# Four fused convolution layers on one core: the half products are issued in pairs, and one without a partner waits for the next quarter

## The chip, the cores and the metric

The kernel runs on one core of one Trainium2 chip. The metric is device microseconds of one execution, lower is better. Three runs of the kernel before gave 2782.89, 2783.59 and 2784.94 us, a median of 2783.59 us.

## The reference

The input is x of 16 images, 64 channels, 128 by 128 pixels, all float32. Four layers follow each other, each of them x = x + f(groupnorm(x)) with 32 groups of two channels:

```
x = x + conv_w @ (gram(xn) @ xn)           # gram = xn xn^T / 16384, 64x64 per image
x = x + |scharr_x(xn)| + |scharr_y(xn)|    # per channel, 3x3
x = x + conv3x3(shifted(xn), W) + b        # a quarter of the channels one pixel left, one right
x = x + clip(leaky(batchnorm(conv1x1(conv3x3(xn, w_bin), w1x1))), 0, 255)
```

The batch norm takes its mean and variance over all 16 images, so the last step of layer 3 can only start when every image has passed the third convolution.

## The kernel before

**Tiles.** A tile holds 128 partitions. In the front (layers 0 and 1) these are 64 channels times the two halves of the image's rows; in the convolutions they are 64 channels times even and odd rows. A tile covers 16 rows, so an image takes NS = 8 steps. The three stages `Front`, `Layer2` and `Layer3` run at the same time on different images, one tile each in a step; `Layer2` is 10 steps and `Layer3` 20 steps behind `Front` (`starts`, line 922). A fourth piece, `Gram`, turns a later image's rows into columns (`rows_to_columns`, ScalarE) and forms the 64x64 Gram matrix with 128 small products of 65 columns (`gram_product`, line 406). From it `gram_chain` computes the coefficients of layer 0 in some nine links, each with small products (`small_product`, line 171) that go into the PSUM tile `bank`; `coefficients` does the same for the group norms of layers 2 and 3 with one small product each. A link of a chain is run by `tick()` at the end of a quarter.

**Order.** A step has four quarters q = 0 to 3. In the loop of line 972 each quarter runs, in this order: the "first of" pieces, `Layer3`, `Layer2` and `Front` for the images that are in them, the "last of 3" piece in quarter 3, `Gram`, and `tick()`. All engines except the queues' own work keep the program's order (`InOrder`, line 63): an instruction never passes another one of its engine in the instruction stream.

**Halves on TensorE.** Almost every product has 128 rows of weights and 64 columns; it writes PSUM partitions 0 to 63 (half 0) or 64 to 127 (half 1). The variable `last[0]` is the half of the last product issued. `small_product` issues one product for each half, beginning with the other half than the last. `issue` (line 652) takes two lists, one for each half, and alternates; when one list is used up it issues the rest of the other.

**A convolution tile.** `shared` issues three products for each half into `one`. `own` (line 672) issues for one of the two output row sets five products into `two`: three taps for one half, and two products for the other, because one of its two is packed with the twin tile `qd` (`pk`). So one half has one product more. For `Layer2`, `own(…, 1, …)` in quarter 2 has the extra product in half 0 and `own(…, 0, …)` in quarter 3 has it in half 1. For `Layer3` the two calls are in quarters 0 (extra in half 0) and 1 (extra in half 1). Line 803 to 825 and 880 to 886 hold these calls.

**The inputs of `own`.** `difference(name, n, t)` (line 634, VectorE) writes `d2[:, n]` or `d3[:, n]`; there is one buffer for each n. The difference of `Layer2` for n = 1 is written in "last of 3" (line 830), at the end of quarter 3, for the next tile; it overwrites what the three taps of quarter 2's `own` read. The twin `qd` is a shifted copy of `d`, made by two transfers from the GpSimd queue for layer 2 and by ScalarE for layer 3.

**Other names of the profile.** `po` is the product of layer 0 for half a tile (quarters 1 and 3), from which ScalarE makes the normalized `xh`. VectorE writes `y` (layer 3's output, quarter 2) from `two` and the bias tile `c`, and `x` written from `two,c` is layer 2's output (quarter 0); `two<-two,edges` are the two border corrections ahead of the latter. The Gram products of an image stand in three parts of 44, 42 and 42 (line 477 and, for images 1 to 6, line 499). For images 7 to 15 the parts are in quarter 0 and 2 of one step and quarter 0 of the next.

**After the convolutions.** When the last tile of layer 3 is done, the batch norm's coefficients are formed, and the loop of line 1056 reads `y_d` and `x3_d` back, applies the last step and writes the output.

All instructions issued through `InOrder` carry line 73 in the profile, so groups are told apart by the tiles that they write and read.

Of the kernel before, what the change touches and what calls it, by code (L numbers as in the profile page):

```python
# [108 lines left out]
def tile_kernel(ctx: ExitStack, tc: tile.TileContext, x, cw_h, w2_t, b2, wbin_t, w1_t, b1, gamma, beta, consts, out):  # L109
    nc = tc.nc  # L110
    pe, dve, act, sp, pool = (InOrder(tc, e) for e in (nc.tensor, nc.vector, nc.scalar, nc.sync, nc.gpsimd))
# [57 lines left out]
    last = [1]  # L169
# [55 lines left out]
    def weights_of_layer_3(ky):  # L225

        pw = bank[C:P, 512 - 3 * C:512].rearrange("p (k c) -> p k c", k=3)
        for kx in range(3):
            pe.matmul(pw[:, kx, :], wb[:, ky, kx, :], w1, start=True, stop=True)
        for slot, i, o, kk in TO_PAIRS:  # L230
            if kk == ky:
                act.copy(w3[i * C:(i + 1) * C, slot, :, o * C:(o + 1) * C], pw)
# [5 lines left out]
    def other_weights():  # L238
        for n in range(2):
            o = 1 - single(TO_SLOTS, n)[0]  # L240
            pool.tensor_copy(wm[:, :, cols(o)], w2[:, n, :, cols(o)])

        for name, w, table in (("pk2", w2, TO_SLOTS), ("pk3", w3, TO_PAIRS)):
            dve.tensor_add(w[:, 2], w[:, 0], w[:, 1])
            packed[name] = wpool.tile([P, 2, C], F32, name=name)
            for n in range(2):
                o, i = single(table, n)
                for kx, half in ((1, i), (0, 1 - i)):
                    pool.tensor_copy(
                        packed[name][half * C:(half + 1) * C, n], w[i * C:(i + 1) * C, n, kx, o * C:(o + 1) * C]  # L250
                    )
# [4 lines left out]
    def tick():  # L256
        for c in list(chains):
            if next(c, chains) is chains:
                chains.remove(c)
# [146 lines left out]
    def gram_product(pg, w):  # L406

        s = w % 2
        pe.matmul(
            pg[s * C:(s + 1) * C, :], xw[:, w // 2, 0:C, s], xw[:, w // 2, :, s],  # L410
            start=(w < 2), stop=(w >= W - 2),
        )
        last[0] = s

    def rows_to_columns(b, m, t):
        act.copy(
            xw[:, :, m * C // 8:(m + 1) * C // 8, :].rearrange("p w c t -> p c w t"),
            t.rearrange("p c (w t) -> p c w t", t=2),
        )
# [38 lines left out]
    class Gram:  # L458
        first, last = 0, NS + 1
# [21 lines left out]
        def part(self, n):  # L481
            if self.w == 0 and n:
                self.pg = ps_g.tile([P, CP, W], F32, tag="g", name=f"pg_{self.b}")[:, 0, 0:C + 1]
            for _ in range(n):
                gram_product(self.pg, self.w)
                self.w += 1

        def load(self, m):
            t = xin.tile([P, C // 8, W], F32, tag="xr", name=f"xr_{self.b}_{m}", bufs=3)
# [17 lines left out]
    class Front:  # L507
        first, last = -3, NS
# [132 lines left out]
    def taps(o, p, wts, srcs, pad=0):  # L641
# [7 lines left out]
                ))  # L649
        return made  # L650

    def issue(halves):

        n = [0, 0]
        while n[0] < len(halves[0]) or n[1] < len(halves[1]):
            o = 1 - last[0]
            if n[o] == len(halves[o]):
                o = last[0]
            dst, wt, src = halves[o][n[o]]
            n[o] += 1  # L660
            pe.matmul(dst, wt, src, start=(n[o] == 1), stop=(n[o] == len(halves[o])))
            last[0] = o

    def products(p, wts, srcs):
        issue([taps(o, p, wts, srcs) for o in range(2)])
# [6 lines left out]
    def own(p, n, table, wt, name, m=CP, both=None):  # L672
        d, q, pk = diffs[name][:, n, 0:m], twins[name][:, n, 0:m], packed[f"pk{name[1]}"][:, n]
        o, _ = single(table, n)
        some = [None, None]
        some[1 - o] = taps(1 - o, p[:, 0:m], [wt[:, n] if both is None else both], [d], 1)
        some[o] = [
            (p[cols(o), 0:m], pk, q[:, :, 1:1 + W]),
            (p[cols(o), 0:m, 0:W - 1], wt[:, n, 2, cols(o)], d[:, :, 2:1 + W]),
        ]  # L680
        issue(some)
# [4 lines left out]
    class Layer2:  # L686
        first, last = -2, NS
# [146 lines left out]
    class Layer3:  # L834
        first, last = -1, NS
# [89 lines left out]
    def run(stage, b, i, q):  # L925
        if 0 <= b < B and stage.first <= i <= stage.last:
            if (stage, b) not in live:
                live[stage, b] = stage(b)
            live[stage, b].at(i, q)
# [20 lines left out]
    def rest(pool, tag, shape, bufs, n=None):  # L950
        for m in range(bufs if n is None else n):
            t = pool.tile([P] + shape, F32, tag=tag, name=f"end_{tag}_{len(room)}", bufs=bufs)
            while len(t.shape) > 2:
                t = t.rearrange("p a b c -> p (a b) c" if len(t.shape) == 4 else "p a b -> p (a b)")
            room.append(t[:, 0:N])

    def slices(t, n):
        room.extend(t[:, j * N:(j + 1) * N] for j in range(n))
# [3 lines left out]
    def fetch():  # L962
        n = fetched[0]
        if n < len(parts):
            b, q = parts[n]
            yt, rt = room.popleft(), room.popleft()
            sp.dma_start(yt, whole(y_d[b], q))
            sp.dma_start(rt, whole(x3_d[b], q))
            loaded.append((yt, rt))
            fetched[0] += 1  # L970

    for step in range(starts[2][1] - 2, steps):
        for q in range(4):
            for b in range(B):

                i = step - starts[2][1] - NS * b
                if 0 <= i < NS and q in (0, 2):
                    live[Front, b].sobel(i, f"first of {q}")
                if q == 3:
                    run(Layer2, b, step - starts[1][1] - NS * b, "first of 3")  # L980
            for stage, at in starts:
                for b in range(B):
                    run(stage, b, step - at - NS * b, q)
            if q == 3:
                for b in range(B):
                    run(Layer2, b, step - starts[1][1] - NS * b, "last of 3")
            for b in range(1, B):
                at, n = pace[b]
                if n == 1:
                    run(Gram, b, step - at, q)  # L990
                elif 0 <= step - at <= 5:
                    live.setdefault((Gram, b), Gram(b)).half(4 * (step - at) + q)

            first = starts[2][1]
            if step == first and q < 3:
                rows_to_columns(1, NS - 3 + q, rows[NS - 3 + q])
            if q == 1 and first + 2 <= step < first + 5:
                weights_of_layer_3(step - first - 2)
            if q == 1 and step == first + 5:
                other_weights()  # L1000
            tick()

            if step == last_one - NS and q == 0:
                slices(xw.rearrange("p w c t -> p (w c t)"), 8)
                slices(xh.rearrange("p a j w -> p (a j w)"), 3)
                rest(xin, "x", [R, W], 2)
                rest(xin, "xr", [C // 8, W], 3)
                rest(work, "u", [R + 1, W + 2], 2)
                rest(work, "e", [R, W + 2], 1)
            if step == last_one and q == 0:  # L1010
                rest(ring, "v2", [(R + 1) * W + 2], 3)
                for t in (diffs["d2"], twins["d2"]):
                    slices(t.rearrange("p n j w -> p (n j w)"), 1)
            if step >= last_one and q == 2:

                n = 3 if step == last_one else 1 if step < last_one + NS - 2 else 0
                rest(ring, "x3", [2, CP, W], NS + 2, n)

            if step >= last_one - NS and q == 3 and len(room) > 1:
                fetch()  # L1020
# [82 lines left out]
```

## Time and profile before

| | |
|---|---|
| median of three runs | 2783.59 us |
| the profiled execution's own time | 2780.96 us |
| its span, first to last instruction | 2779.2 us |
| TensorE matmul busy | 2220.0 us (80%) |
| VectorE busy | 2193.7 us (79%) |
| ScalarE busy | 2113.9 us (76%) |
| GpSimd busy | 837.1 us (30%) |
| products of 64 columns, rows of the profile | 14804, two for each product |
| last product of the convolutions | near 2326 us of the span |
| from there to the end | reading back, last step, writing out |

The busy shares are those of the whole span. From about 316 us (first tile of layer 3) to about 2053 us all three stages run; the profile before that is the filling of the pipeline, after it the emptying. From 2340 us on TensorE is idle and the 16 transfer engines are fully busy (414 GB/s). A timeline row gives the start, the length, the engine, the operation, the tiles, the shape, the number of merged instructions and, in brackets, the engine's idle time before it and what ended it. A product leaves two rows, one for each of two passes; the length of a row includes about 0.16 us in which the next product already runs, so the start of the next row tells more than the length.

### The profile page before, as it was taken

The numbers are of one execution on the slowest core, as the hardware profiler recorded it, in microseconds if no ns is written. First come the engines' busy times: TensorE is split into PE (matmuls) and PEld (weight loads), VectorE is DVE, ScalarE is ACT, GpSimd is POOL, SyncE is SP. The second block draws the span as 40 slices with busy tenths as digits, with TensorE's granted clock in tenths as the row PEclk, the third lists the DMA queues.
The fourth block names the chain that finished last, engine by engine and source line by source line (L and its number), as shares of the span: only waits on it lengthen the run. The fifth ranks groups of instructions, "written<-read, shape, count | busy, mean of one in ns | idle before, by whom it ended". The sixth has DMA issues, their size and how long they took to land. (4 is left out here: it accounts for less than half of the span.)

```text
span 2779.2 us, 46241 instructions
## 1 busy us (share of the span) xinstructions
PE 2220.0 (80%) x14804; PEld 1125.6 (41%) x14804; DVE 2193.7 (79%) x3623; ACT 2113.9 (76%) x3177; POOL 837.1 (30%) x1350
## 2 busy tenths in 40 slices
PE   6478899999999999999999999999999995000000
PEld 4234444545454535453535353566666641000000
DVE  5999999898989898989898989999996435333332
ACT  4766889898989898989898988999997667333332
POOL 2054434332333242324242424444444300000000
PEclk8689999999999999999999999999999997555555
DMA  7789888888888888888888867787877768999999
GB/s 200 201 226 233 231 208 232 227 220 221 216 227 223 221 221 222 220 227 215 226 218 223 218 181 204 205 215 208 213 201 188 216 192 285 419 420 420 420 420 390
DMA packets 680289, 685.97 MB, mean 247 GB/s; under 512 B 60096, under 2 KB 580448, under 8 KB 680048
## 3 DMA queue, kind: packets, MB, share of 16 engines
q1 hardware_dynamic: 654896, 613.83, 74.5%
q0 software_dynamic: 25152, 69.18, 10.2%
q8 instruction: 120, 1.97, 0.3%
q14 instruction: 121, 0.99, 0.1%
HBM read 346.23 MB, written 268.44 MB: 221 GB/s over the span
## 5 line engine op out<-in xcount | busy, mean ns | idle before, releaser
L73 PE MATMUL two<-d,w 128*64 128x508 f32 (+2 forms) x2560 | 884.4, 586 | 0.0
L73 PE MATMUL two<-d,wi 128*64 128x508 f32 (+3 forms) x1536 | 616.6, 577 | 0.0
L73 POOL DMA_DIRECT2D qd<-d x512 | 270.8, 531 | 900.5 <-issue 382.2
L73 PE MATMUL two<-qd,pk 128*64 128x512 f32 (+1 forms) x1024 | 518.2, 587 | 5.9 <-DMA qd<-d 5.4
L73 POOL TENSOR_SCALAR edges<-v,co 64x8 f32<-64x8 f32 x512 | 308.4, 602 | 370.4 <-ACT v L73 276.3
L73 PEld LDWEIGHTS two<-d,w 128*64 128x64 f32 x2560 | 299.3, 136 | 279.9 <-issue 202.8
L73 PE MATMUL one<-v,wi 128*64 128x508 f32 (+3 forms) x1536 | 396.6, 596 | 2.5 <-issue 2.5
L73 PE MATMUL one<-v,w 128*64 128x508 f32 (+2 forms) x1600 | 398.1, 578 | 0.5 <-ACT c L73 0.5
L73 PE MATMUL po<-x,abd 128*64 128x512 f32 x1024 | 351.9, 617 | 51.9 <-ACT xh L73 48.9
L73 DVE TENSOR_TENSOR d<-v 128x512 f32<-128x512 f32 (+1 forms) x512 | 346.0, 679 | 38.6 <-ACT qd L73 14.2
L73 ACT COPY qd<-d 64x512 f32<-64x512 f32 x512 | 315.4, 616 | 21.1 <-DVE d L73 14.6
L73 ACT ACTIVATE xh<-po,co 128x128 f32<-128x128 f32 (+1 forms) x480 | 275.1, 621 | 63.7 <-PE po L73 60.5
L73 DVE SCALAR_TENSOR_TENSOR e<-e 128x1032 f32<-128x1032 f32 (+1 forms) x256 | 313.0, 1223 | 0.0
L73 DVE SCALAR_TENSOR_TENSOR y<-two,c 128x1024 f32<-128x1024 f32 x128 | 156.0, 1219 | 133.5 <-ACT v L73 66.4
L73 PEld LDWEIGHTS two<-d,wi 128*64 128x64 f32 x1536 | 193.9, 135 | 153.0 <-issue 109.9
L73 ACT ACTIVATE v<-x,co 128x512 f32<-128x512 f32 (+2 forms) x368 | 234.9, 704 | 0.0
L73 PEld LDWEIGHTS one<-v,w 128*64 128x64 f32 x1600 | 162.3, 137 | 176.3 <-issue 119.7
L73 POOL TENSOR_SCALAR v<-v,kc 128x9 f32<-128x9 f32 x256 | 228.2, 905 | 11.9
L73 PEld LDWEIGHTS one<-v,wi 128*64 128x64 f32 x1536 | 157.2, 139 | 161.6 <-issue 120.0
L73 ACT ACTIVATE u<-u 128x1024 f32<-128x1024 f32 x128 | 135.1, 1055 | 65.3 <-DVE u L73 65.3
L73 DVE SCALAR_TENSOR_TENSOR u<-xh 128x1170 f32<-128x1170 f32 x128 | 175.6, 1372 | 4.7 <-ACT xh L73 3.8
L73 PEld LDWEIGHTS two<-qd,pk 128*64 128x64 f32 x1024 | 130.2, 136 | 111.6 <-issue 72.1
(162 smaller groups left out, 3453.8 us busy)
## 6 DMA issues: line engine op xcount, KB each, us to landing
x<-in_x SPq DMA_DIRECT2D x256, 256.0 KB, 4.0
x_d<-u SPq DMA_DIRECT2D x512, 128.0 KB, 3.7
y_d<-y SPq DMA_DIRECT2D x512, 128.0 KB, 4.1
x_d<-x SPq DMA_DIRECT2D x496, 128.0 KB, 2.5
xr<-in_x SPq DMA_DIRECT2D x120, 512.0 KB, 6.5
qd<-d POOLq DMA_DIRECT2D x256, 130.0 KB, 3.0
qd<-d POOLq DMA_DIRECT2D x256, 129.8 KB, 3.7
v<-x_d SPq DMA_DIRECT2D x448, 72.1 KB, 3.0
```

The costliest lines, as they stand in the source:

```text
L73: return self.tc.keep_in_program_order(call(*args, **kwargs))
```

## The change

`issue` no longer issues everything. Each half has a queue (`held`). `issue` puts its products at the end of the queues, with their start and stop flags, and then issues pairs, one product for each half, as long as both queues hold something. A product without a partner stays in its queue until the next `issue`. Before `Front` in quarters 1 and 3 `issue_rest` would empty the queues. The parts of the Gram are issued in pairs that begin with the other half than the last.

```diff
-            for _ in range(n):
-                gram_product(self.pg, self.w)
-                self.w += 1
+            for _ in range(n // 2):
+                for s in (1 - last[0], last[0]):
+                    gram_product(self.pg, self.w + s)
+                self.w += 2
...
+    held = [deque(), deque()]
+
+    def emit(o):
+        dst, wt, src, start, stop = held[o].popleft()
+        pe.matmul(dst, wt, src, start=start, stop=stop)
+        last[0] = o
+
     def issue(halves):
 
-        n = [0, 0]
-        while n[0] < len(halves[0]) or n[1] < len(halves[1]):
+
+        for o in range(2):
+            for n, (dst, wt, src) in enumerate(halves[o]):
+                held[o].append((dst, wt, src, n == 0, n + 1 == len(halves[o])))
+        while held[0] and held[1]:
             o = 1 - last[0]
-            if n[o] == len(halves[o]):
-                o = last[0]
-            dst, wt, src = halves[o][n[o]]
-            n[o] += 1
-            pe.matmul(dst, wt, src, start=(n[o] == 1), stop=(n[o] == len(halves[o])))
-            last[0] = o
+            emit(o)
+            emit(1 - o)
+
+    def issue_rest():
+        while held[0] or held[1]:
+            emit(1 - last[0] if held[1 - last[0]] else last[0])
...
             for stage, at in starts:
+                if stage is Front and q in (1, 3):
+                    issue_rest()
                 for b in range(B):
                     run(stage, b, step - at - NS * b, q)
```

The number of instructions on every engine stays the same, and the order on VectorE, ScalarE, GpSimd and the queues too. On TensorE the third product of `own` in quarters 0 and 2 now stands behind the Gram part and the small products of that quarter's `tick()`, as the first product of the next quarter; where nothing stands between, the order of products is the one of before.

## The prediction

> **What bounds the kernel now.** First the stretches with the busy time of each engine, to see where TensorE sets the pace.
>
> ```profile
> 400.00:600.00 200.00, 198.88 (x1268) 100.22 (x1265) 188.15 (x324) 181.56 (x284) 74.79 (x123) 1.00 0.88 231
> 1805.00:1929.00 124.00, 124.00 (x630) 79.93 (x628) 120.70 (x180) 113.95 (x181) 57.57 (x82) 1.00 0.82 210
> 2340.00:2780.00 440.00, 0.00 (x0) 0.00 (x0) 149.35 (x124) 149.50 (x122) 0.00 (x0) 0.50 1.01 414
> ```
>
> The columns are length, busy us of TensorE, weight loads, VectorE, ScalarE and GpSimd, granted clock, share of the transfer engines, GB/s. TensorE is busy all the time until the last 440 us, which transfers bound and the change doesn't touch. VectorE is busy 188 of 200 us, so a gain on TensorE may end at VectorE. So I read VectorE's waits next, around one image's Gram steps (first tile of layer 3 of that image at 860.7 us).
>
> ```profile
> 919.30 1.23 DVE L73 SCALAR_TENSOR_TENSOR y<-two,c 128x1024 f32<-128x1024 f32 x1 [1.16 <-ACT u L73]
> 924.49 0.69 DVE L73 TENSOR_TENSOR d<-v 128x512 f32<-128x512 f32 x1 [0.36 <-issue]
> 929.58 0.38 DVE L73 TENSOR_TENSOR two<-two,edges 128x8 f32<-128x8 f32 x2 [1.95 <-PE two L73]
> 939.98 1.23 DVE L73 SCALAR_TENSOR_TENSOR y<-two,c 128x1024 f32<-128x1024 f32 x1 [3.43 <-ACT junk L73]
> 945.38 0.56 DVE L73 TENSOR_TENSOR d<-v 128x384 f32<-128x384 f32 x1
> DVE d L73 <- POOL v L73: 0.4, 2, 0.2
> ```
>
> The last row is the whole list of VectorE's waits from 946 to 1055 us: 0.4 us. The image's period is 136.3 us (724.4, 860.7, 997.0 us). So it has two parts: TensorE leads up to 940 us, where VectorE waits up to 3.43 us for it; then VectorE runs without a pause for more than 100 us, and TensorE waits for it through ScalarE (`po` behind `xh`, 1.2 us at 876.7). Time is saved only if both parts hand on earlier.
>
> **Part 1: the lone product.** How TensorE treats a product without a partner:
>
> ```profile
> 1001.23 0.23 PE L73 MATMUL bank<-st,kc 128*64 128x2 f32 x2
> 1001.32 1.05 PE L73 MATMUL two<-d,w 128*64 128x512 f32 x3
> 1002.08 0.22 PE L73 MATMUL bank<-st,kc 128*64 128x2 f32 x2
> ...
> 912.93 0.34 PE L73 MATMUL pg<-xw 128*64 128x65 f32 x2
> 913.35 0.59 PE L73 MATMUL two<-d,w 128*64 128x508 f32 x1
> 913.78 2.92 PE L73 MATMUL pg<-xw 128*64 128x65 f32 x86
> 916.48 0.59 PE L73 MATMUL two<-d,w 128*64 128x512 f32 x1
> 916.53 0.59 PE L73 MATMUL two<-qd,pk 128*64 128x512 f32 x1
> ```
>
> A small product of half 1 runs at 1001.23 beside the lone product of half 0 (two passes of 0.427 us, 0.854 in all). Half 1 goes on with its next long product at 1001.32; the small one of half 0, earlier in the program, runs only at 1002.08. The halves are two streams; each loses 0.085 us at the small product and 0.033 in the long one behind it (second pass at 1001.78, 0.46 later instead of 0.427), 0.118 us.
>
> The page "TensorE: Matmul & The Clock Gate" of the Trainium skill, Part 3, says that matmuls start and end strictly in program order. By it each of the 55 small groups and 34 Gram parts that stand behind a lone product would idle a half for up to 0.854 us, and the change would gain up to 89 × 0.854 / 2 = 38 us. The rows at 1001.32 and 1002.08 contradict it, and the sum goes by them.
>
> Small products between pairs, with the halves level:
>
> ```profile
> 324.06 0.28 PE L73 MATMUL bank<-ad,cs 128*64 128x64 f32 x4
> 324.18 0.23 PE L73 MATMUL bank<-vv,abd 128*64 128x2 f32 x4
> 324.27 0.26 PE L73 MATMUL bank<-vv,wbd 128*64 128x1 f32 x4
> 324.38 1.91 PE L73 MATMUL one<-v,wi 128*64 128x512 f32 x8
> ```
>
> Three of them take 324.06 to 324.38, with the late second pass 0.356 us, against 3 × 0.118 = 0.354. So I cost moving the 55 groups at 0. Bounds: nothing, and each 0.118 dearer (the halves' small products one after the other), 55 × 0.118 = +6.5 us.
>
> **Part 2: the Gram parts.** A Gram part is not free behind a lone product: half 1 makes one Gram product at 912.93 and then waits until half 0 has finished its long one. It spends 912.93 to 916.48 = 3.55 us on 22 products; half 0 takes 913.78 to 916.53 = 2.75. So half 1 loses 0.80 us, half 0 nothing. In the changed kernel both do the part from 912.93 to 915.68, and then the pairs. Half 0 is where it was, half 1 0.80 earlier. The image's two later parts lose nothing in either half (926.82 and 926.85), as half 0 is then ahead by that much.
>
> `y` needs both halves. At 919.30 it could go 0.80 earlier (VectorE is free at 918.14), and at 939.98 0.81. This would be the gain.
>
> **Part 3: what waits for the held product.** The difference at 924.49 overwrites what the held product reads. That product runs from 923.39 (last row end 924.40, and 0.09 to the difference). Now it stands behind the Gram part of 42, 2.64 us (924.19 to 926.82): end 927.04, difference 927.13, 2.64 later. Behind it on VectorE stand `u` and `e` (3.12 us up to the end of `e`), so `two<-two,edges`, held by TensorE until 929.58, starts at 930.25: 0.67 late. The 6.98 us of work up to the next `y` then ends at 937.2, before TensorE's 939.17. The 3.43 us of wait shrink to 1.9: no cost. GpSimd's transfers behind this difference (`qd`) are 2.6 us later and are read some 15 us later: no cost.
>
> But the next difference, at 945.38, has no wait and no room. The product it overwrites is of half 0: second pass at 944.59, end 945.17, with 0.09 it is free at 945.26. Half 0 is not earlier in the changed kernel. So VectorE, 0.81 early at `y`, waits here for 0.69 and keeps 0.12. From here to 1055 us VectorE has no slack: 0.12 is what the image hands on. Nine images have this pattern (`y` with a wait near 509.6, 646.7 and so on to 1601.4): 9 × −0.12 = −1.1 us. Bounds: 0, and 9 × −0.81 = −7.3.
>
> **Part 4: the filling (166 to 370 us).** Images 4 to 6 have Gram parts in quarter 2 beside layer 2 while `y` isn't there. At 203.31 the difference waits for GpSimd; its lone product starts at 201.39. Held behind 2.75 us of Gram it ends at 205.16, the difference goes at 205.25, 1.94 late, and `two<-two,edges` goes at 208.4 instead of 207.71: +0.7. A second part of the image adds about as much, some 1.3 us an image. In the last of the three `y` waits 3.06 us for TensorE (at 345.5), which should take it back. So 2 × 1.3 = +2.6 us; bounds 0 and 3 × 1.3 = +3.9.
>
> **Part 5: elsewhere 0.** From 1680 to 2250 us no Gram is left. TensorE is the bound (124.00 of 124.00), both halves' work stays the same, and small products cost the same 0.118 in either place. In the emptying nothing stands between the quarters' products, so the order is unchanged.
>
> **Sum.** −1.1 + 2.6 = +1.5 us. The profiled execution took 2780.96 us (span 2779.2 and 1.8 around it), which makes 2782.5. The median of the runs is 2.6 above that execution: 2785.1 us.
>
> **Rivals.**
> *Faster: half 1's 0.8 us is handed on whole.* For it: `y` waits on TensorE, and half 1 is the later one in every Gram step. Against it: the end of half 0's product at 945.17, 0.2 us ahead of the difference. If the differences held nothing up and the filling cost nothing, −7.3: 2776.3 us.
> *Slower: the held product stops VectorE for good.* Place: the difference behind the Gram part in quarter 2, 2.64 us late. It decides from the point where `y` at 939.98 has no wait left, or where ScalarE, behind VectorE's `u`, is late with `xh` and so with `po`. Then the 0.67 us at 929.58 stay in all nine images, 6.0 us, with 2.6 of the filling +8.6: 2792.2 us. Against it: 1.9 us of wait remain by my walk.
> *The change does less than it says.* Where no Gram or chain link stands between two quarters the order is unchanged, and if the waits take both signs back the time is 2783.6; this lies within my forecast.
>
> **How the numbers follow.** 0.2% is 5.6 us, about what a measurement of this kernel can tell from no change. No change within it: 0.62 (2778.0 to 2789.2). Faster: 0.17. Slower: 0.21, with the dearer small products (+6.5) in it. The forecast's own range is 2782 to 2788: filling 0 to +3.9, images 0 to −1.1, and a run's spread of 1 us. The range of 8 in 10 reaches to both rivals: 2776 to 2792.
>
> **What would show it.** In the changed profile: each Gram part in one row of 84 or 88 products, with no long product inside; `y` about 0.7 us earlier in the period than now with a wait of about 2 us at the second one; a wait of about 0.7 us at the difference that follows it; a wait of some 3 us at the difference behind the Gram part in quarter 2; periods of 136.2 us. I am wrong if the period moves by more than 0.5 us, if steps without Gram take more than 15.4 us, or if three small products between pairs take more than 0.36 us.

## The result, and the profile after

| | runs | median us | lowest to highest |
|---|---|---|---|
| kernel before, beside it | 12 | 2782.92 | 2779.74 to 2784.94 |
| changed kernel | 12 | 2782.61 | 2778.85 to 2784.50 |

The ratio is 0.9999, 95% interval 0.9991 to 1.0006: no change that can be told. The profiled execution of the changed kernel took 2783.50 us, its span 2781.7 us.

First the stretches with the busy time of each engine, of the changed kernel (columns as before):

```profile
400.00:600.00 200.00, 197.14 (x1262) 93.91 (x1260) 188.41 (x323) 183.57 (x286) 76.83 (x122) 1.00 0.88 232
1805.00:1929.00 124.00, 124.00 (x630) 80.05 (x628) 120.78 (x179) 113.99 (x182) 56.78 (x83) 1.00 0.81 210
2340.00:2780.00 440.00, 0.00 (x0) 0.00 (x0) 151.77 (x126) 151.93 (x125) 0.00 (x0) 0.50 1.02 416
```

VectorE's 188 of 200 us, TensorE's 124.00 of 124.00 without Grams and the end are what they were. Over the whole span TensorE is busy 2209.7 us instead of 2220.0 with the same 14804 rows. Two halves that are level cover less time than two of which one lags, which would fit; no run shows this by itself.

TensorE's timeline of the changed kernel around an image's Gram parts (first tile of layer 3 of this image at 1000.9 us):

```profile
1052.36 1.02 PE L73 MATMUL two<-d,w 128*64 128x508 f32 x4
1053.21 2.92 PE L73 MATMUL pg<-xw 128*64 128x65 f32 x88
1055.96 1.44 PE L73 MATMUL two<-d,w 128*64 128x512 f32 x5
...
1063.66 2.80 PE L73 MATMUL pg<-xw 128*64 128x65 f32 x84
1066.30 1.02 PE L73 MATMUL two<-d,wi 128*64 128x512 f32 x4
```

Each part is one row of 88 or 84 entries (44 or 42 products) with no long product inside. From its start to the next product the larger part takes 2.75 us and the smaller one 2.64, in both halves. Half 1's 3.55 us are gone. The held product is now the first of its half behind the part, in the row at 1066.30; its second pass ends at 1067.32.

VectorE's timeline of the changed kernel through the same steps, and from its list of waits the rows for the 106 us behind them:

```profile
1058.81 1.23 DVE L73 SCALAR_TENSOR_TENSOR y<-two,c 128x1024 f32<-128x1024 f32 x1 [0.38 <-ACT v L73]
...
1067.41 0.69 DVE L73 TENSOR_TENSOR d<-v 128x512 f32<-128x512 f32 x1 [3.74 <-issue]
...
1070.46 0.38 DVE L73 TENSOR_TENSOR two<-two,edges 128x8 f32<-128x8 f32 x2
...
1079.44 1.22 DVE L73 SCALAR_TENSOR_TENSOR y<-two,c 128x1024 f32<-128x1024 f32 x1 [2.01 <-ACT e L73]
...
1085.54 0.56 DVE L73 TENSOR_TENSOR d<-v 128x384 f32<-128x384 f32 x1 [0.61 <-issue]
DVE d L73 <- POOL v L73: 0.4, 2, 0.2
```

The waits of this image have moved from `y` and the border corrections to the two differences: 3.74 us at the one behind the Gram part, which starts 0.09 us after the end of the held product, 2.01 instead of 3.40 at the second `y`, and a new one of 0.61 at the next difference. Set against the same instructions of the kernel before, matched one by one, VectorE in the changed kernel is later by:

| place in the image | us later | change |
|---|---|---|
| before the first `y` | 3.99 | |
| first `y` | 3.18 | -0.81 |
| difference behind the Gram part | 6.60 | +2.61 against the start |
| border corrections | 4.55 | +0.56 against the start |
| second `y` | 3.17 | -0.82 against the start |
| the next difference, and on to 1116 us | 3.86 | -0.13 against the start |
| from 1117 us to the next image | 3.78 | -0.21 handed on |

0.8 us comes in at `y`, 0.13 is left behind the next difference, and 0.21 leaves the image. The other 0.08 comes at an instruction of the chain (`wbd<-bank,r`), which waits 0.04 us instead of 0.11 in all nine images. The period, from `y` to `y` in images without a stray wait, is 136.08 us instead of 136.29.

The small products between pairs (changed kernel, TensorE's timeline):

```profile
326.57 0.28 PE L73 MATMUL bank<-ad,cs 128*64 128x64 f32 x4
326.69 0.23 PE L73 MATMUL bank<-vv,abd 128*64 128x2 f32 x4
326.77 0.26 PE L73 MATMUL bank<-vv,wbd 128*64 128x1 f32 x4
326.89 2.34 PE L73 MATMUL one<-v,wi 128*64 128x512 f32 x10
```

Three take 326.57 to 326.89, 0.32 us, as in the kernel before, where these three also stood between pairs. One that has moved there takes 0.09 us in both halves (1005.21 to 1005.30).

### The profile page after: what moved, and what is told of

It reads as the page before. It is cut to its first block, busy times and chain, and to the rows that moved or that the text cites. A ratio compares the mean times of both kernels' runs of the same rounds, so it can differ in the third digit from the quotient of the medians.

```text
span 2781.7 us, 46232 instructions
## 1 busy us (share of the span) xinstructions
PE 2209.7 (79%) x14804; PEld 1118.6 (40%) x14804; DVE 2193.6 (79%) x3623; ACT 2116.5 (76%) x3177; POOL 867.2 (31%) x1350
## 5 line engine op out<-in xcount | busy, mean ns | idle before, releaser
L73 PE MATMUL two<-d,w 128*64 128x508 f32 (+2 forms) x2560 | 854.3, 587 | 0.0
L73 PE MATMUL two<-d,wi 128*64 128x508 f32 (+3 forms) x1536 | 583.9, 578 | 0.0
L73 POOL TENSOR_SCALAR edges<-v,co 64x8 f32<-64x8 f32 x512 | 324.7, 634 | 345.1 <-ACT v L73 253.5
L73 PEld LDWEIGHTS two<-d,w 128*64 128x64 f32 x2560 | 290.5, 136 | 267.7 <-issue 185.4
L73 PE MATMUL one<-v,w 128*64 128x508 f32 (+2 forms) x1600 | 371.5, 578 | 0.4 <-ACT c L73 0.4
L73 PE MATMUL one<-v,wi 128*64 128x508 f32 (+3 forms) x1536 | 366.0, 595 | 2.7 <-issue 2.7
L73 PE MATMUL po<-x,abd 128*64 128x512 f32 x1024 | 294.6, 616 | 50.8 <-ACT xh L73 47.7
L73 POOL TENSOR_SCALAR v<-v,kc 128x9 f32<-128x9 f32 x256 | 241.9, 959 | 12.0
L73 PEld LDWEIGHTS two<-d,wi 128*64 128x64 f32 x1536 | 182.9, 136 | 143.7 <-issue 100.6
L73 PEld LDWEIGHTS one<-v,wi 128*64 128x64 f32 x1536 | 149.5, 139 | 164.5 <-issue 117.3
```

The costliest lines, as they stand in the source:

```text
L73: return self.tc.keep_in_program_order(call(*args, **kwargs))
```

## The experiments

All are compared with runs of the kernel before on the same chip. "Handed on" is how much earlier VectorE is, against the same instructions of the kernel before or of the named control, over the nine images from 400 to 1700 us.

**Is it the buffer? The changed kernel with a second buffer.** Layer 2's difference for n = 1 gets a second buffer, used in turn with the first, so that it need not wait for the held product that reads the old one.

```diff
+    d2_other = wpool.tile([P, CP, W + 2], F32, name="d2o")
+    pool.memset(d2_other, 0.0)
+    turn2 = [0]
+    def d_of(name, n):
+        if name == "d2" and n == 1 and turn2[0]:
+            return d2_other
+        return diffs[name][:, n]
...
+        if name == "d2" and n == 1:
+            turn2[0] = 1 - turn2[0]
-        dve.tensor_sub(diffs[name][:, n, 0:m, 1:1 + W], (after if n else even)[:, 0:m], odd[:, 0:m])
+        dve.tensor_sub(d_of(name, n)[:, 0:m, 1:1 + W], (after if n else even)[:, 0:m], odd[:, 0:m])
```

> The changed kernel with a second buffer for layer 2's difference of n = 1, used in turn, so that the difference no longer overwrites what the held product reads. Theory (the 0.8 us that half 1 gains in each Gram part stops at this difference): the wait of 3.7 us behind the Gram part and the one of 0.6 us after the second y vanish, each of the nine images with Gram parts takes about 135.6 us instead of 136.1, the filling loses its 2.5 us, together 8 to 10 us faster than the kernel before (ratio near 0.9967). Rival (half 1's gain is worth nothing, since both halves carry the same work and half 0 is no earlier): no faster than before apart from the filling, ratio 0.999 or more.

Measured: 2778.47 us, ratio 0.9986 (0.9977 to 0.9995). Both new waits of the differences are gone and the steady period is 135.4 to 135.5 us. But the gain, 4.2 us, is little more than half of nine times 0.8 us. The control is the same buffer in the kernel before:

> The kernel before with the same second buffer, the control of the first run. Theory: in the kernel before the difference waits only 0.36 us behind the Gram part and not at all after the second y, and half 1 is still 0.8 us behind, so about 1 us faster, not to be told from no change. Rival (the buffer alone is the gain, whatever the order of the products): as fast as the first run, 8 to 10 us faster.

Measured: 2786.0 us, ratio 1.0013 (1.0004 to 1.0022): the buffer alone made the kernel before 3.4 us slower, with its periods unchanged (136.2 to 136.3). Between the two runs with the buffer lie 7.5 us. 2.8 us of it lay at the end: 451.3 us from the last product to the end instead of 448.5. (The first 47 us may have a share; they scatter by more than 1 us between executions.) The new tile of 2080 bytes in each partition, 32 more than eight times 256, stood ahead of the tiles that transfers fill, and moved them all.

**The same two with the buffer behind all other tiles.**

```diff
+    other = ctx.enter_context(tc.tile_pool(name="other", bufs=1))
...
-    d2_other = wpool.tile([P, CP, W + 2], F32, name="d2o")
+    d2_other = other.tile([P, CP, W + 2], F32, name="d2o")
```

> The changed kernel with the second buffer for layer 2's difference n = 1, allocated behind all other tiles, so that no other tile changes its address. Theory (the extra 3 us of the two earlier runs with a second buffer came from the 32 bytes by which it moved the tiles that transfers fill and empty): periods of an image 135.4 to 135.6 us as in the first of those runs, the first and last part of the span as long as in the changed kernel without it, and 9 x 0.7 = 6 to 8 us less than the kernel before: ratio 0.9971 to 0.9978. Rival (the buffer itself costs 3 us, by its clearing or by the other tile's port): ratio 0.9986, as in the first of those runs.

> The kernel before with the same second buffer behind all other tiles. Theory (the move of the tiles cost the 3 us): ratio 1.000 within 0.0008, period 136.2 to 136.3 us, since there the difference behind the Gram part never waited for the buffer long enough to matter. Rival (the buffer itself costs it): ratio 1.0013.

Measured: the changed kernel with it 2774.37 us, ratio 0.9968 (0.9956 to 0.9981); the kernel before with it 2782.22 us, ratio 0.9998 (0.9989 to 1.0006). Both are as the theory said, the first a little faster than its range: the buffer costs nothing in this place and gains nothing in the kernel before; with the pairs it makes 8.1 us, the fastest of the kernels here together with one further below. VectorE's timeline in it, through one image's steps:

```profile
916.87 1.23 DVE L73 SCALAR_TENSOR_TENSOR y<-two,c 128x1024 f32<-128x1024 f32 x1 [0.71 <-ACT v L73]
...
921.70 0.68 DVE L73 TENSOR_TENSOR d2o<-v 128x512 f32<-128x512 f32 x1
...
927.17 0.38 DVE L73 TENSOR_TENSOR two<-two,edges 128x8 f32<-128x8 f32 x2 [2.34 <-PE two L73]
...
937.52 1.22 DVE L73 SCALAR_TENSOR_TENSOR y<-two,c 128x1024 f32<-128x1024 f32 x1 [3.38 <-ACT junk L73]
...
942.91 0.56 DVE L73 TENSOR_TENSOR d<-v 128x384 f32<-128x384 f32 x1
```

Neither difference waits. The second `y` again waits 3.38 us for TensorE's work, and VectorE's 0.8 us stay: against the control with the same buffer it goes from 1.49 us late at 400 us to 5.49 early at 1700 us, 6.98 us handed on (6.0 to 7.2 when the traces of the other kernels with the old order are taken as the control). In the changed kernel with one buffer the same sum is 0.58.

**Which product must be held?** First the same held in quarter 0 alone: quarter 2's product goes out at once, ahead of the Gram part.

```diff
-                if stage is Front and q in (1, 3):
+                if stage is Front and q in (1, 2, 3):
```

> The changed kernel, but what is held in quarter 2 goes out ahead of Front in that quarter, so that only layer 3's product of quarter 0 is held. Theory: the difference behind the Gram part of quarter 2 is as early as before (its wait of 3.7 us is below 0.6), the filling's 2.5 us are gone (the first tile of layer 3 near 316 us), but half 1 now loses its 0.8 us in the Gram part of quarter 2, so the image takes 136.3 to 136.6 us; total within 2 us of the kernel before. Rival (the late difference of quarter 2 costs the nine images something): faster than the changed kernel by 0.67 us an image, 6 us.

Measured: 2785.8 us, ratio 1.0012 (1.0004 to 1.0021), period 136.7 us, a little outside what was expected. TensorE's timeline in it, an image's two parts:

```profile
916.01 2.94 PE L73 MATMUL pg<-xw 128*64 128x65 f32 x88
...
926.48 0.59 PE L73 MATMUL two<-d,wi 128*64 128x508 f32 x1
926.49 0.41 PE L73 MATMUL pg<-xw 128*64 128x65 f32 x4
926.90 0.59 PE L73 MATMUL two<-d,wi 128*64 128x508 f32 x1
927.33 2.66 PE L73 MATMUL pg<-xw 128*64 128x65 f32 x78
929.78 0.59 PE L73 MATMUL two<-d,wi 128*64 128x512 f32 x1
```

The part of quarter 0 is clean, but in quarter 2 half 1 now makes its first two Gram products (four rows at 926.49) and stops until half 0 is through its lone product. (Which half a row belongs to follows from the program's order.) In the kernel before half 0 was ahead by then, so that its lone product ended when half 1's last one did, and nothing was lost there; now the halves come level, and half 1 loses 926.49 to 929.78 less the 2.62 us of half 0, 0.67 us. The expected wait was missed too: the difference behind this part waits 1.1 us and not less than 0.6, since VectorE comes 0.8 earlier and half 0's product doesn't. Next the reverse: quarter 2's held, quarter 0's not.

```diff
-                if stage is Front and q in (1, 3):
+                if stage is Front and q in (0, 1, 3):
```

> The changed kernel, but layer 3's third product of quarter 0 is issued at once, before the Gram part, as in the kernel before; only quarter 2's product is held. Theory (a half can run just one product beyond one of the other half that is blocked): half 1 loses 0.7 to 0.8 us again in the Gram part of quarter 0, nothing is gained at the first y, and the held product behind the part of quarter 2 is still 2.6 us later for the difference: period 136.4 to 136.7 us, 1 to 5 us over the kernel before. Rival (each half just runs its own products and order doesn't matter): 136.0 as in the changed kernel, no difference.

Measured: 2787.86 us, ratio 1.0020 (1.0011 to 1.0029), 5.4 us over the kernel before, period 136.7 us: the theory's direction, and a little more than its figures. The same view, quarter 0's part:

```profile
917.18 0.41 PE L73 MATMUL pg<-xw 128*64 128x65 f32 x4
917.61 0.59 PE L73 MATMUL two<-d,w 128*64 128x508 f32 x1
918.03 2.82 PE L73 MATMUL pg<-xw 128*64 128x65 f32 x82
920.63 0.59 PE L73 MATMUL two<-d,w 128*64 128x512 f32 x1
```

Half 1 takes 917.18 to 920.63, 3.45 us, and the held product behind the second part still stops the difference (a wait of 3.6 us there). Holding one of the two is worse than holding both or none.

**The small products.** The changed kernel, but the lone product is issued just before the quarter's small products; it still stands behind the Gram part.

```diff
+            issue_rest()
             tick()
```

> The changed kernel, but what is held goes out after the Gram part and ahead of the chains' small products, which so stand behind a lone product as before, while Gram parts stand between pairs. Theory (a small product costs 0.118 us in either place): the same time as the changed kernel within 1 us, images of 136.1 us. Rival (small products between pairs cost up to 0.118 us more each and eat a gain of the Gram parts): faster than the changed kernel by up to 6 us, mostly from steps with links of the chains.

Measured: 2783.02 us, ratio 1.0001 (0.9992 to 1.0010), period 136.2 us. Where the small products stand costs and gains nothing that the times can tell. The traces show the 0.08 us of an image that were named above: `wbd<-bank,r` waits 0.11 us again.

**The filling.** The changed kernel, and the one with two buffers, but a lone product goes out at once until layer 3's first step.

```diff
-                if stage is Front and q in (1, 3):
+                if stage is Front and (q in (1, 3) or step < starts[0][1]):
```

> The changed kernel, but until the first step of layer 3 a lone product goes out at once, as in the kernel before; from there on it is held. Theory (holding costs about 2 us in the filling, the start's scatter of about 1 us taken off, and gains 0.25 us in each of nine images later): from an instruction at 150 us to the first y nothing is lost against the kernel before (0.3 us at most, where the changed kernel loses 1.9), periods 136.0 to 136.1; ratio to the kernel before 0.9985 to 0.9995. Rival (the filling's loss is not the held product's): first y as late as in the changed kernel, ratio 0.9999.

> The same with the second buffer for layer 2's difference n = 1 behind all other tiles. Theory: as the fastest run so far, and about 1 us less from the filling: ratio 0.9962 to 0.9967, periods 135.4 to 135.6. Rival (no gain left in the filling with two buffers): ratio 0.9968.

Measured: 2781.88 us, ratio 0.9995 (0.9986 to 1.0004), and 2774.50 us, ratio 0.9967 (0.9955 to 0.9980). By the times neither is told from the kernel without the edit. In the traces, from VectorE's first `u` (near 46 us) to the first `y`:

| | us |
|---|---|
| six kernels that issue as before in the filling's quarter 2: the one before, those of the controls and moved tiles | 280.3 to 282.7, mean 281.9 |
| held in quarter 2: the changed kernel, smalls behind, quarter 2 alone | 283.3, 283.3, 283.2 |
| held in quarter 0 alone | 281.9 |
| the changed kernel with the filling as before | 282.0 |
| with two buffers: held, as before in the filling | 281.4, 280.8 |

So holding with one buffer costs some 1.4 us here, though single executions of the same order scatter by 2.4 us; the edit takes it back. From 150 us on the edited kernel loses 0.6 us to the first `y` against the one trace of the kernel before, where I expected 0.3 at most; with that scatter one trace can't test it.

**The moved tiles.** The kernel before, with an unused tile of 32, 256 or 512 bytes for each partition in the first place of the second buffer.

```diff
+    pad = wpool.tile([P, 8], F32, name="pad")
+    pool.memset(pad, 0.0)
```

> The kernel before with an unused tile of 32 bytes for each partition at the place where the first runs had the second buffer; every later tile moves by 32 bytes, and nothing else changes. Theory (transfers to and from SBUF are slower where a tile's address is 32 bytes past a multiple of 256 or 512): as the kernel before with the second buffer in that place: the part after the last product 451.2 us instead of 448.5, the start 0.8 to 2 us longer, 3 to 4 us in all, ratio 1.0011 to 1.0014. Rival (it was the buffer's size or its clearing): ratio 1.000 within 0.0008, 448.5 us after the last product.

> The same with 256 bytes. Theory (a multiple of 256 is enough): 448.5 us after the last product, ratio 1.000 within 0.0008. Rival (a multiple of 512 is needed): 451 us after the last product, 3 to 4 us in all.

> The same with 512 bytes. Theory (the address against a multiple of 256 or 512 decides): 448.5 us after the last product, ratio 1.000 within 0.0008. Rival (any move from the given addresses costs it): 451 us after the last product.

| tiles moved by | us | ratio (interval) | last product to end, us |
|---|---|---|---|
| 32 | 2786.74 | 1.0012 (1.0003 to 1.0021) | 451.4 |
| 256 | 2782.87 | 1.0000 (0.9991 to 1.0009) | 448.3 |
| 512 | 2783.12 | 1.0000 (0.9992 to 1.0009) | 448.7 |

32 bytes cost what the misplaced buffer had cost; 256 and 512 cost nothing. It wasn't the buffer's size or its clearing.

## Why the prediction was right

The forecast (no change, 2785.1 us, range 2776 to 2792) held, and the walk through the image held link by link. In the filling one link of it failed, and both sums were off in size, so that the closeness of the time itself shows little.

- **Part 1, small products at 0.** Right within 1 us: one that moved takes 0.09 us, as its two halves did before, and the run with the small products behind the lone one is at 1.0001. Their place is worth 0.08 us of each of the nine images, a term that the prediction didn't have. The 38 us from strict program order were nowhere.
- **Part 2, half 1's 0.80 us.** Right: both halves take 2.75 us for the larger part, and `y` is 0.81 earlier in its image.
- **Part 3, the differences.** Predicted against the start of the image: difference 2.64 late, corrections 0.67 late, `y` 0.81 early with 1.9 us of wait left, the next difference waiting 0.69, 0.12 handed on. Measured in the image shown: 2.61, 0.56, 0.82, 2.01, 0.61, 0.13. The runs with two buffers show that these waits keep the gain: without them 6.98 us are handed on, where the rival *faster* had 9 × 0.81 = 7.3.
- **The size of Part 3's sum** was small: nine images handed on 1.9 us and not 1.1, 0.21 each, of which 0.13 is the predicted term and 0.08 the one that was missing. The kernel with the filling as before goes from 1.23 late at 400 us to 0.72 early at 1700 (between 1.2 and 2.5 us in all when the other traces with the old order are the control). Taken at the difference behind the second `y` of each image, where the prediction counts, seven of its eight steps from image to image give 0.12 to 0.27 us and one gives 0.48.
- **Part 4, the filling.** The mechanism is right for the first two images: the difference predicted to go 1.94 late goes 1.92 late, the corrections 0.57 late (predicted 0.7), both less the 0.6 us by which this execution was late before. VectorE's timeline of the kernel before, then of the changed one:

```profile
203.31 0.69 DVE L73 TENSOR_TENSOR d<-v 128x512 f32<-128x512 f32 x1 [0.93 <-POOL v L73]
...
207.71 0.38 DVE L73 TENSOR_TENSOR two<-two,edges 128x8 f32<-128x8 f32 x2 [1.26 <-PE two L73]
```

```profile
205.83 0.69 DVE L73 TENSOR_TENSOR d<-v 128x512 f32<-128x512 f32 x1 [2.84 <-issue]
...
208.88 0.38 DVE L73 TENSOR_TENSOR two<-two,edges 128x8 f32<-128x8 f32 x2
```

  The sizes were off in two ways that nearly cancel. The two images cost 1.9 us between these two profiles, not 2.6, and some 1.4 against the mean of the other traces. The third was to give its loss back at the `y` of 345.5 us and didn't: that `y` is 1.28 us less late, but the difference behind it then waits 3.36 us, and layer 3's first image, which runs beside it, takes 136.7 to 136.8 us in the three traces that hold both products here with one buffer, instead of 136.2 to 136.3 in four with the old order. That makes 2.5 us up to 400 us in these two profiles, and some 1.9 over all traces.
- **Part 5, elsewhere 0.** Steps without a Gram are 15.40 us as before, and the end 448.6 against 448.5.
- **The sum.** Between the two profiled executions +1.5 was predicted and +2.5 measured: 0.6 from the start, which varies between executions of one kernel by more than that, 1.9 to the first `y`, 0.5 in layer 3's first image, -1.9 from the images, and +1.4 from one stray step of 20.1 us (17.1 in the other images). Over all traces, and without the stray step, the terms are +1.4, +0.5 and -1.9, together nothing; the runs' medians differ by -0.3 us, with an interval of -2.5 to +1.7. So both terms of the sum were too high, and both lie within the bounds that the prediction gave them (0 to +3.9 and 0 to -7.3).
- **The median.** 2785.1 took over the 2.6 us by which the first three runs' median lay above the profiled execution. Twelve runs of the kernel before have a median of 2782.92: 0.7 of the 2.5 us between forecast and result is this, and not the kernel; the other 1.8 is the sum, +1.5 against -0.3.
- **The rivals.** *Slower* decides where `y` has no wait left; 2.0 us were left, 1.9 predicted. It came about in another way when only one of the two products was held. *Does less than it says* is refuted by the waits that moved; that its time was right is the trap of a result of 1.000.

## What to carry to other kernels

A change that ends at 1.000 may hold a gain and a stop that cancel: follow one instruction of the bounding engine through a period, and look at which single-buffered tile the reordered product still reads; here a second buffer of 2080 bytes in each partition turned 0 into 8 us. Where an order keeps two streams in step, its parts only pay together: holding one of two lone products was slower than neither or both. Put a trial buffer behind all other tiles, or its effect is mixed with that of moving them.

## What the hardware showed that was not expected

**The address of a tile at the start of a partition's row matters to transfers.** Moved by 32 bytes, the same bytes took 451.4 us instead of 448.5 behind the last product, 0.6% more; moved by 256 or 512 they took 448.3 and 448.7. The page "DMA: Bandwidth & Descriptors" of the Trainium skill, section "How a descriptor splits into AXI transactions", says that a transaction starts at a multiple of 256 bytes and that bytes fetched ahead of the start cost beats of 32 bytes. For 512 KB over 128 partitions, 4096 bytes each, an estimate by it is 129 beats instead of 128, 0.8% or 3.5 us, if loads and stores pay alike. The runs gave 2.9 us, and agree that 256 is enough. The single packets don't show the estimate's size: from 60 to 400 us behind the last product those of 4096 bytes took 159.5 ns instead of 159.1, 0.3%. Up to the last 100 packets 1.1 of the 2.9 us was lost, and these 100 lost the rest; why they did is open. Between 32 and 256 bytes nothing was tried.

**How far a half runs ahead.** Beside the other half's lone product, half 1 made one Gram product in the kernel before, where the part begins with half 0, and two where the part begins with half 1 (four rows at 917.18 and at 926.49). Both times it stopped one product beyond the first of half 0 that couldn't start. So in these rows the halves are two streams, and one of them may run a single product beyond a blocked one of the other.

**A stray long step.** Two executions have one step, from layer 3's first product in a tile to that in the next, about 3 us longer than its likes in the other images (20.14 against 17.13 us in the changed kernel, 19.77 against 16.97 with the second buffer in its first place), half or most of it kept. What it is stays open; spans of single executions of this kernel can't be compared to the microsecond.
